# Layer 0's gate with stationary weights in four column groups of TensorE, turned by two transposes

## The chip, the cores and the metric

The kernel runs on one core of one Trainium2 chip. The metric is the device time of one execution in microseconds. The kernel before takes 3072.12 us, the median of three runs (3068.05 to 3079.04).

## What is computed

A stack of four graph layers on 16 graphs of 1024 nodes with 128 features, each followed by a residual addition and a layer norm. The change concerns layer 0, a gated attention over the graph:

```python
h = x @ W_w.T + W_b
e = jnp.einsum('bjl,bkl->bjk', h @ A, h)
e = e + jnp.swapaxes(e, 1, 2)
att = jnp.where(adj > 0, e, jnp.float32(-9000000000000000.0))
att = jax.nn.softmax(att, axis=1) * adj
h_prime = jax.nn.relu(jnp.einsum('bij,bjk->bik', att, h))
coeff = jax.nn.sigmoid(jnp.concatenate([x, h_prime], axis=-1) @ gate_w.T + gate_b)
return coeff * x + (1.0 - coeff) * h_prime
```

The gate `coeff` is one number per node: a dot product of 256 values, 128 of them from the node's input and 128 from its attention result.

## The kernel before, in words

`fast_kernel` runs the layers one after the other: layer 0, the dilation of the adjacency matrices, the three graph convolutions of layer 1, and layers 2 and 3. Layer 0 goes through 16 graphs ("batches"), each in three streams, which `in_turn` interleaves, so that in the steady state three batches are in work at once: `before` of batch b+1, `attention` of batch b, `after` of batch b−1. The tile framework then fixes the order of the instructions on each engine when the program is built; on the chip each engine takes its instructions in that order, and semaphores hold an instruction until what it needs is there.

`before` (line 891 on) has eight steps, one for each block of 128 adjacency rows `an`. ScalarE casts the block and sums it (`ab`, line 900), VectorE checks it (`chk`, line 903, in a buffer of its own of 1024 bytes per partition), TensorE turns it by eight transposes (`pt`, line 907), and VectorE writes it as a mask (`carry`, line 908). Between these steps come the products: the turned input `xT` (step 1), `hT` from `W0T` and the gate's first half `pz` with its copy `gx` (step 3), `G` (step 5), `hn` (step 7).

`attention` (line 933 on) has eight steps jt: a mask on ScalarE (`msk`, line 942), the scores `pmm` on TensorE (line 723), mask and maximum on VectorE (`em`, line 945), the exponential on ScalarE (line 949), `rs` and `hs` on VectorE (lines 951 and 953), and `acc` on TensorE (line 956).

`after` (line 959 on) forms `hpT`, the ReLU of `acc`, on ScalarE, then the gate's second half `pz` (line 965), adds `gx` (`co`, line 967), takes a tanh, and mixes input and result (`xn`, `r`, lines 974 to 977), before the layer norm (lines 777 to 784, with a power on GpSimd at line 744).

The gate's product has the node features stationary and the weight vector moving: for each of the eight blocks of 128 nodes, one matmul loads 128x128 float32 values and streams a single column. It gives 128 nodes on the partitions and 8 columns, which is how `co` is used.

`ps_h` is a pool of PSUM with two buffers under the one tag "h". The products, `pt`, the turned tiles and the gate all take turns in it: the third tile waits until the first is read. `ps_w` has two buffers for the scores `pmm`, `ps_a` one for `acc`.

`bad` (line 675) collects the dilation's flags, which are 0 or 1; the end of the kernel takes their maximum.

Of the kernel before, what the change touches and what calls it, by code (L numbers as in the profile page):

```python
# [9 lines left out]
F32 = mybir.dt.float32  # L10
F16 = mybir.dt.float16
F32R = mybir.dt.float32r
BF16 = mybir.dt.bfloat16
I32 = mybir.dt.int32
I8 = mybir.dt.int8
FP8 = mybir.dt.float8e4
# [6 lines left out]
P = 128  # L23
# [616 lines left out]
def fast_kernel(ctx: ExitStack, tc: tile.TileContext, t: dict, out: bass.AP, flag: bass.AP):  # L640

    nc = tc.nc
    B, N, D = t["x"].shape
    NT = N // P
# [3 lines left out]
    consts = ctx.enter_context(tc.tile_pool(name="consts", bufs=1))  # L648
    dram = ctx.enter_context(tc.tile_pool(name="dram", bufs=1, space=DRAM))

    identf = consts.tile([P, P], F32, name="identf")
# [20 lines left out]
    deg = consts.tile([P, BT], F32, name="deg")  # L672
    dinv = deg

    bad = consts.tile([P, 2, NT, B], F32, name="bad")
    past = consts.tile([P, NT - 2, B], F32, name="past")
    other = consts.tile([P, BT], F32, name="other")

# [82 lines left out]
    def products(psum, *pairs):  # L761

        for p, c, _ in halves(psum):
            for i, (W, x) in enumerate(pairs):
                nc.tensor.matmul(p, W, x[:, c], start=(i == 0), stop=(i == len(pairs) - 1))  # L765
            yield p, c

    def half_rows(v):

        return v[:, :, None].to_broadcast([P, 4, P])  # L770
# [97 lines left out]
    with ExitStack() as ph:  # L868

        early = ph.enter_context(tc.tile_pool(name="l0_early", bufs=1, reuse_waits="tile"))  # L870
        wts = ph.enter_context(tc.tile_pool(name="l0_w", bufs=1, reuse_waits="tile"))
        ps_w = ph.enter_context(tc.tile_pool(name="l0_pw", bufs=2, space=PSUM, reuse_waits="tile"))
        ps_a = ph.enter_context(tc.tile_pool(name="l0_pa", bufs=1, space=PSUM, reuse_waits="tile"))
        ps_h = ph.enter_context(tc.tile_pool(name="l0_ph", bufs=2, space=PSUM, reuse_waits="tile"))

        with tc.tile_pool(name="l0_raw", bufs=1) as raw:
            W0T = transposed(wts, ps_h, matrix(raw, t["L0_gnn_W_w"], "l0W"), "l0WT", "h")
            As0 = symmetric(wts, ps_h, matrix(raw, t["L0_gnn_A"], "l0A"), "l0As", "h")
        work = ph.enter_context(tc.tile_pool(name="l0_work", bufs=1, reuse_waits="tile"))
        small = ph.enter_context(tc.tile_pool(name="l0_small", bufs=2, reuse_waits="tile"))  # L880
        b0 = column(wts, t["L0_gnn_W_b"], "l0b")
        gw = wts.tile([P, 2], F32, name="l0gw")
        with nc.allow_non_contiguous_dma(reason="a vector of 256"):
            nc.sync.dma_start(gw, t["L0_gnn_gate_w"].rearrange("o (h d) -> d (o h)", d=P))
        gb = row_bcast(wts, t["L0_gnn_gate_b"], 1, "l0gb")
        gbh = wts.tile([P, 1], F32, name="l0gbh")
        nc.vector.tensor_scalar(gbh, gb, 0.5, None, op0=OP.mult)
        nbig = wts.tile([P, 1], F32, name="l0nbig")
        nc.vector.memset(nbig, -BIG)

        def before(s, b):

            s.xn = work.tile([P, NT, P], F32, name="xn", bufs=3)
            nc.sync.dma_start(s.xn, nat(t["x"][b]))
            for it in range(NT):
                c = b * NT + it
                an = early.tile([P, N], F32, name="an", bufs=2)
                nc.sync.dma_start(an, t["adj"][b][it * P:(it + 1) * P, :])
                ab = early.tile([P, N], BF16, name="ab", bufs=2)
                nc.scalar.activation(ab, an, AF.Copy, accum_out=deg[:, c:c + 1])  # L900

                chk = early.tile([P, N], FP8, name="chk")
                nc.vector.scalar_tensor_tensor(chk, an, 0.0, an, op0=OP.is_gt, op1=OP.not_equal,  # L903
                                               accum_out=other[:, c:c + 1], saturate=False)
                pt = ps_h.tile([P, NT, P], BF16, name="pt", tag="h")
                for jt in range(NT):
                    nc.tensor.transpose(pt[:, jt, :], ab[:, jt * P:(jt + 1) * P], identb)  # L907
                nc.vector.tensor_scalar(Y[b][:, :, it * P:(it + 1) * P], pt, 0.0, None, op0=OP.is_gt, saturate=False)  # L908
                if it == 1:
                    xT = early.tile([P, N], F32, name="xT")  # L910
                    for p, c, _ in turned(ps_h, s.xn):
                        nc.scalar.copy(xT[:, c], p)
                elif it == 3:
                    s.hT = work.tile([P, N], F32, name="hT", bufs=2)
                    for p, c in products(ps_h, (W0T, xT)):
                        nc.scalar.activation(s.hT[:, c], p, AF.Identity, bias=b0)
                    pz = ps_h.tile([P, NT], F32, name="pz", tag="h")
                    for i in range(NT):
                        nc.tensor.matmul(pz[:, i:i + 1], xT[:, i * P:(i + 1) * P], gw[:, 0:1], start=True, stop=True)
                    s.gx = small.tile([P, NT], F32, name="gx")  # L920
                    nc.vector.tensor_copy(s.gx, pz)
                elif it == 5:
                    s.G = work.tile([P, N], F32, name="G", bufs=2)
                    for p, c in products(ps_h, (As0, s.hT)):
                        nc.scalar.copy(s.G[:, c], p)
                elif it == 7:
                    s.hn = work.tile([P, N], F32, name="hn")
                    for p, c, _ in turned(ps_h, s.hT):
                        nc.vector.tensor_copy(s.hn[:, c], p)
                yield  # L930
            nc.gpsimd.dma_start(adj8_d[b], Y[b].bitcast(F32))

        def attention(s, b):


            s.acc = ps_a.tile([P, N], F32, name="acc")
            for jt in range(NT):
                js = slice(jt * P, (jt + 1) * P)
                c = b * NT + jt
                mx = mx0[:, c:c + 1]  # L940
                msk = work.tile([P, N], BF16, name="msk", bufs=2)
                nc.scalar.activation(msk, Y[b][:, jt, :], AF.Identity, scale=BIG, bias=nbig)  # L942
                e = wide_matmul(ps_w, s.hT[:, js], s.G)
                em = work.tile([P, N], F32, name="em", bufs=2)
                nc.vector.tensor_tensor_reduce(em, e, msk, 1.0, -3.0e38, op0=OP.add, op1=OP.max, accum_out=mx)  # L945
                nmx = small.tile([P, 1], F32, name="nmx")
                nc.vector.tensor_scalar(nmx, mx, -1.0, None, op0=OP.mult)  # L947
                sm = small.tile([P, 1], F32, name="sm")
                nc.scalar.activation(em, em, AF.Exp, bias=nmx, accum_out=sm)  # L949
                rs = small.tile([P, 1], F32, name="rs")  # L950
                nc.vector.reciprocal(rs, sm)
                hs = small.tile([P, P], F32, name="hs")
                nc.vector.tensor_scalar(hs, s.hn[:, js], rs, None, op0=OP.mult)  # L953
                for h in range(H2):
                    c = slice(h * 512, (h + 1) * 512)
                    nc.tensor.matmul(s.acc[:, c], hs, em[:, c], start=(jt == 0), stop=(jt == NT - 1))  # L956
                yield

        def after(s, b):

            hpT = work.tile([P, N], F32, name="hpT")
            nc.scalar.activation(hpT, s.acc, AF.Relu)
            pz = ps_h.tile([P, NT], F32, name="pz", tag="h")
            for i in range(NT):
                nc.tensor.matmul(pz[:, i:i + 1], hpT[:, i * P:(i + 1) * P], gw[:, 1:2], start=True, stop=True)
            co = small.tile([P, NT], F32, name="co")
            nc.vector.tensor_add(co, pz, s.gx)
            nc.scalar.activation(co, co, AF.Tanh, scale=0.5, bias=gbh)
            cx = small.tile([P, NT], F32, name="cx")
            nc.vector.tensor_scalar(cx, co, 0.5, 1.5, op0=OP.mult, op1=OP.add)  # L970
            nc.vector.tensor_scalar(co, co, -0.5, 0.5, op0=OP.mult, op1=OP.add)
            yield
            r = work.tile([P, NT, P], F32, name="r")
            nc.vector.tensor_mul(s.xn, s.xn, per_row(cx))
            for p, c, k in turned(ps_h, hpT):
                nc.vector.tensor_mul(r[:, k, :], tiles3(p), half_rows(co[:, k]))
            nc.vector.tensor_add(s.xn, s.xn, r)
            yield
            normed(small, s.xn)
            nc.gpsimd.dma_start(nat(x1_d[b]), s.xn)  # L980
            yield

        in_turn(before, attention, after)
# [712 lines left out]
```

## Time and profile before

| what | value |
|---|---|
| time, median of 3 | 3072.12 us |
| profiled span | 3066.2 us |
| PE, DVE, ACT busy over the span | 93%, 76%, 66% |
| gate of line 919, matmuls | 256 x 245 ns, 29.5 us |
| gate of line 965, matmuls | 256 x 247 ns, 30.0 us |
| `gx` and `co` on VectorE | 16 each, 167 ns |
| layer 0 | about the first 760 us |

PE is TensorE's matmuls and PEld its weight loads, DVE VectorE, ACT ScalarE, POOL GpSimd. A row of the profile names the line, the engine, the tile that is written and the tiles that are read. [...] A float32 matmul appears as two loads and two matmuls. The chain of work that ended last shows each piece with its start and its share of the chain, without overlap.

### The profile page before, as it was taken

How to read it: one execution, taken by the hardware profiler on the slowest of the kernel's cores; microseconds unless marked ns; L12 is line 12 of the kernel's file. 1: busy time of each engine (PE TensorE's matmuls, PEld its weight loads, DVE VectorE, ACT ScalarE, POOL GpSimd, SP SyncE). 2: the span in 40 equal slices, each digit the busy share in tenths (PEclk: the TensorE clock that was granted, in tenths of full speed). 3: DMA queues.
4: the chain of work that ended last, by engine and by line, in shares of the span. 5: the costliest groups of instructions: out<-in, count | busy, mean ns of one | idle time of the engine just before them, and what ended most of it. 6: DMA issues, size and time to landing. Idle time of an engine off the chain costs nothing.

```text
span 3066.2 us, 43116 instructions
## 1 busy us (share of the span) xinstructions
PE 2848.6 (93%) x15379; PEld 1834.6 (60%) x15442; DVE 2327.7 (76%) x5971; ACT 2015.0 (66%) x3393; POOL 314.6 (10%) x292
## 2 busy tenths in 40 slices
PE   7999999997899999999999987999999999999995
PEld 4454554554566566777788874555655555555554
DVE  7788888886899996676678885766667677767765
ACT  6677777775678877565555534766666666666753
POOL 0000000003000001111122231000000000000000
PEclk9999999998899999999999997999999999999997
DMA  5344344331000014223366793111121121111000
GB/s 188 117 139 149 132 138 151 131 131 49 2 2 2 1 79 162 83 93 122 122 218 226 251 331 113 35 56 62 55 69 55 63 74 63 55 55 56 21 14 22
DMA packets 123216, 297.98 MB, mean 97 GB/s; under 512 B 12656, under 2 KB 64624, under 8 KB 115824
## 3 DMA queue, kind: packets, MB, share of 16 engines
q1 hardware_dynamic: 102384, 211.13, 20.6%
q0 software_dynamic: 20608, 84.00, 7.4%
q8 instruction: 124, 2.03, 0.3%
q14 instruction: 100, 0.82, 0.1%
HBM read 211.04 MB, written 84.02 MB: 96 GB/s over the span
## 4 chain that ended last, share of the span: by engine, by line
PE 60%; issue 17%; DVE 13%; ACT 3%; POOL 3%; DMA 3%; SPq 0%; POOLq 0%; DVEq 0%; ACTq 0%
PE pmm L723 10%; PE acc L1272 9%; PE ph L1515 7%; PE ph L765 6%; PE acc L1578 6%; PE acc L956 5%; PE ph L758 4%; PE ph L1376 4%; PE ph L1501 2%; POOL ln_rstd L744 2%; DVE ln_st L777 2%; PE acc L1249 2%; ACT xn L784 1%; DVE chk L903 1%; PE pt L907 1%
## 5 line engine op out<-in xcount | busy, mean ns | idle before, releaser
L723 PE MATMUL pmm<-G,hT 128*128 128x512 f32 x1024 | 518.9, 624 | 17.0 <-DVE mx L945 14.7
L723 PEld LDWEIGHTS pmm<-G,hT 128*128 128x128 f32 x1024 | 182.1, 198 | 180.6 <-issue 113.6
L1578 PE MATMUL acc<-em,hs 128*128 128x512 f32 x512 | 255.2, 610 | 12.1 <-DVE hs L1575 10.5
L956 PE MATMUL acc<-em,hs 128*128 128x512 f32 x512 | 239.0, 603 | 23.7 <-DVE hs L953 22.4
L784 ACT ACTIVATE xn<-xn,ln_nb,ln_rstd 128x128 f32<-128x128 f32 x512 | 206.4, 481 | 79.7 <-DVE ln_nb L782 79.7
L1272 PE MATMUL acc<-a,lo 128*128 128x512 f32 x768 | 241.1, 398 | 2.0 <-DVE lo L1240 2.0
L1272 PE MATMUL acc<-a,hi 128*128 128x512 f32 x768 | 241.8, 399 | 1.2 <-ACT hi L1239 0.9
L744 POOL TENSOR_TENSOR ln_rstd<-ln_rstd,mhalf 128x8 f32<-128x8 f32 x64 | 105.4, 1647 | 1295.2 <-DVE ln_rstd L741 1224.6
L1121 ACT ACTIVATE q<-s,negc 128x512 f16<-128x512 f32 x256 | 170.6, 697 | 58.4 <-DVE negc L1100 22.3
L1119 PE MATMUL s<-step,carry 128*128 128x384 bf16 (+3 forms) x1034 | 199.0, 303 | 7.5 <-DVE carry L1089 3.2
L1564 DVE CUSTOM_DVE_ANT_0 em<-pmm,msk 128x1024 f32<-128x1024 f32 x128 | 156.0, 1219 | 50.2 <-PE pmm L723 47.5
L1133 ACT ACTIVATE carry<-pc,negone 128x512 fp8e4<-128x512 f32 x256 | 166.8, 699 | 37.1 <-PE pc L1132 27.8
L903 DVE SCALAR_TENSOR_TENSOR chk<-an 128x1024 fp8e4<-128x1024 f32 x128 | 156.2, 1220 | 38.3 <-DMA an<-in_adj 37.7
L900 ACT ACTIVATE ab<-an 128x1024 bf16<-128x1024 f32 x128 | 134.6, 1052 | 74.9 <-PE pt L907 36.1
L956 PEld LDWEIGHTS acc<-em,hs 128*128 128x128 f32 x512 | 93.5, 191 | 140.8 <-issue 104.9
L1559 ACT ACTIVATE msk<-A,nbig 128x1024 bf16<-128x1024 fp8e4 x128 | 146.0, 1141 | 47.9 <-DVE mx L1564 46.0
L942 ACT ACTIVATE msk<-carry,l0nbig 128x1024 bf16<-128x1024 fp8e4 x128 | 145.5, 1140 | 46.0 <-DVE mx L945 41.5
L908 DVE TENSOR_SCALAR carry<-pt 128x1024 fp8e4<-128x1024 bf16 x128 | 155.9, 1220 | 23.6 <-PE pt L907 23.5
L1272 PEld LDWEIGHTS acc<-a,lo 128*128 128x128 f32 x768 | 142.8, 188 | 42.9 <-DVE lo L1240 9.5
L1272 PEld LDWEIGHTS acc<-a,hi 128*128 128x128 f32 x768 | 141.6, 188 | 34.0 <-ACT hi L1239 1.4
L945 DVE CUSTOM_DVE_ANT_0 em<-pmm,msk 128x1024 f32<-128x1024 f32 x128 | 155.4, 1214 | 5.4 <-PE acc L956 3.3
L949 ACT ACTIVATE em<-em,nmx 128x1024 f32<-128x1024 f32 x128 | 145.9, 1140 | 17.3 <-DVE nmx L947 13.5
(278 smaller groups left out, 6519.9 us busy)
## 6 DMA issues: line engine op xcount, KB each, us to landing
an<-in_adj SPq DMA_DIRECT2D x128, 512.0 KB, 3.3
adj_d<-carry POOLq DMA_DIRECT2D x16, 1024.0 KB, 4.9
A<-dil_d SPq DMA_DIRECT2D x16, 1024.0 KB, 6.5
rdeg<-rdeg_d SPq DMA_DIRECT2D x32, 512.0 KB, 4.3
ag_d<-ag POOLq DMA_DIRECT2D x32, 512.0 KB, 5.3
ag<-ag_d SPq DMA_DIRECT2D x32, 512.0 KB, 6.2
A<-adj_d SPq DMA_DIRECT2D x16, 1024.0 KB, 4.8
xn<-in_x SPq DMA_DIRECT2D x16, 512.0 KB, 3.7
```

Of the source, the lines that this page charges most:

```text
L723: nc.tensor.matmul(p[:, h * 512:(h + 1) * 512], lhsT, rhs[:, h * 512:(h + 1) * 512], start=True, stop=True)
L744: nc.gpsimd.tensor_tensor(r, r, mhalf[:, :n], op=OP.pow)
L765: nc.tensor.matmul(p, W, x[:, c], start=(i == 0), stop=(i == len(pairs) - 1))
L784: nc.scalar.activation(r[:, i, :], r[:, i, :], AF.Identity, scale=rstd[:, i:i + 1], bias=nb[:, i:i + 1])
L903: nc.vector.scalar_tensor_tensor(chk, an, 0.0, an, op0=OP.is_gt, op1=OP.not_equal, accum_out=other[:, c:c + 1], saturate=False)
L956: nc.tensor.matmul(s.acc[:, c], hs, em[:, c], start=(jt == 0), stop=(jt == NT - 1))
L1119: nc.tensor.matmul(s[:, lo or 0:], y, twos if lo is None else step[:, :512 - lo], start=(j == 0), stop=(j == len(terms) - 1))
L1121: nc.scalar.activation(q[:, h * 512:(h + 1) * 512], s, AF.Abs, bias=st.negc[:, i:i + 1])
L1133: nc.scalar.activation(Y[b][:, hb, ks], pc, AF.Relu, bias=negone, saturate=False)
L1272: nc.tensor.matmul(acc, part[:, jt, :], pieces[h * NT // 2 + i][:, j, :], start=(jt == 0 and p == 0), stop=(jt == NT - 1 and p == 1))
L1515: nc.tensor.matmul(p, part[:, jt, :], A[:, jt, c], start=(jt == 0 and i == 0), stop=(jt == NT - 1 and i == 1))
L1578: nc.tensor.matmul(s.acc[:, c], hs, em[:, c], start=(jt == 0), stop=(jt == NT - 1))
```

## The change

The gate is turned around. Its weight vector becomes the stationary operand: `gw` grows from two columns to two blocks of 32 columns, of which the first holds the weights and the others are zero. The features become the moving operand. The new helper `gates` gives each quarter of the 1024 nodes to one column group of TensorE, by `tile_position`: four matmuls of 32 stationary columns and 256 moving columns write to partitions 0, 32, 64 and 96 of one PSUM tile (`pq`). ScalarE copies that tile to SBUF; two transposes bring the nodes back to the partitions (`pg`), and `gx` and `co` read column 0 of each group. The copy takes the buffer of `chk` in `before` and that of `r` in `after`, and `bad` becomes bfloat16, so that no more SBUF is needed.

It is meant to replace eight loads of 128x128 stationary values, each for one moving column, by four matmuls side by side.

```diff
-    bad = consts.tile([P, 2, NT, B], F32, name="bad")
+    bad = consts.tile([P, 2, NT, B], BF16, name="bad")
...
+    def gates(psum, out, *pairs):
+        p = psum.tile([P, N // 4], F32, name="pq", tag="h")
+        for i, (g, x) in enumerate(pairs):
+            for q in range(4):
+                nc.tensor.matmul(p[32 * q:32 * q + 32, :], g, x[:, q * N // 4:(q + 1) * N // 4], start=(i == 0),
+                                 stop=(i == len(pairs) - 1), tile_position=(0, 32 * q))
+        nc.scalar.copy(out, p)
+        p = psum.tile([P, 2, P], F32, name="pg", tag="h")
+        for t in range(2):
+            nc.tensor.transpose(p[:, t, :], out[:, t * P:(t + 1) * P], identf)
+        return p.rearrange("p t (q g) -> p q t g", q=4)
...
-        gw = wts.tile([P, 2], F32, name="l0gw")
+        gw = wts.tile([P, 2, 32], F32, name="l0gw")
+        nc.vector.memset(gw, 0.0)
...
-                    pz = ps_h.tile([P, NT], F32, name="pz", tag="h")
-                    for i in range(NT):
-                        nc.tensor.matmul(pz[:, i:i + 1], xT[:, i * P:(i + 1) * P], gw[:, 0:1], start=True, stop=True)
+                    pz = gates(ps_h, early.tile([P, N], FP8, name="chk").bitcast(F32), (gw[:, 0, :], xT))
                     s.gx = small.tile([P, NT], F32, name="gx")
-                    nc.vector.tensor_copy(s.gx, pz)
+                    nc.vector.tensor_copy(s.gx.rearrange("p (q t) -> p q t", t=2), pz[:, :, :, 0])
...
-            pz = ps_h.tile([P, NT], F32, name="pz", tag="h")
-            for i in range(NT):
-                nc.tensor.matmul(pz[:, i:i + 1], hpT[:, i * P:(i + 1) * P], gw[:, 1:2], start=True, stop=True)
+            pz = gates(ps_h, work.tile([P, NT, P], F32, name="r").rearrange("p t d -> p (t d)")[:, :N // 4], (gw[:, 1, :], hpT))
             co = small.tile([P, NT], F32, name="co")
-            nc.vector.tensor_add(co, pz, s.gx)
+            nc.vector.tensor_add(co.rearrange("p (q t) -> p q t", t=2), pz[:, :, :, 0],
+                                 s.gx.rearrange("p (q t) -> p q t", t=2))
```

More of the change, by code (lines that the diff above doesn't have):

```diff
@@ L881, in fast_kernel @@
         b0 = column(wts, t["L0_gnn_W_b"], "l0b")
-        gw = wts.tile([P, 2], F32, name="l0gw")
+        gw = wts.tile([P, 2, 32], F32, name="l0gw")
+        nc.vector.memset(gw, 0.0)
         with nc.allow_non_contiguous_dma(reason="a vector of 256"):
-            nc.sync.dma_start(gw, t["L0_gnn_gate_w"].rearrange("o (h d) -> d (o h)", d=P))
+            nc.sync.dma_start(gw[:, :, 0], t["L0_gnn_gate_w"].rearrange("o (h d) -> d (o h)", d=P))
         gb = row_bcast(wts, t["L0_gnn_gate_b"], 1, "l0gb")
```

## The prediction

> **What bounds the kernel now.** The change touches layer 0 only, so I first ask where layer 0 is and what limits it. The answer by windows shows five alike stretches of 100 us between 150 and 650 us, at full TensorE clock:
>
> ```profile
> 250.00:350.00 100.00, 93.86 (x426) 50.57 (x425) 85.82 (x203) 76.21 (x126) 6.88 (x7) 1.00 0.41 140
> 350.00:450.00 100.00, 94.14 (x429) 51.25 (x428) 85.43 (x204) 75.50 (x123) 6.33 (x6) 1.00 0.41 140
> ```
>
> Columns are busy us of PE, PEld, DVE, ACT and POOL. TensorE is 94% busy, VectorE 85%, ScalarE 76%: three engines close together, so what a TensorE saving is worth depends on the waits between them. Next, the chain of work that ended last, for one batch (the gate of line 965 starts at 400.83 and again at 446.02, so a batch takes 45.19 us):
>
> ```profile
> 400.83 1.68 PE pz L965 x16
> 402.51 0.48 PE pt L907 x8
> ...
> 403.01 1.23 DVE carry L908
> ...
> 418.53 1.23 DVE chk L903 x2
> ...
> 420.30 3.67 PE acc L956 x8
> 423.97 1.68 PE pz L919 x16
> 425.65 0.47 PE pt L907 x8
> ...
> 440.58 3.43 PE acc L956 x8
> 444.04 1.98 PE pmm L723 x4
> ```
>
> The reader should see two halves. From 403.0 to 420.3 the chain runs through VectorE; from 420.3 to 446 and on to 403 it is TensorE back to back, and both gates (1.68 us each) stand in that half. The third view is VectorE's waits in the same batch:
>
> ```profile
> DVE chk L903 <- DMA an<-in_adj: 3.1, 3, 1.3
> DVE carry L908 <- PE pt L907: 1.3, 3, 0.8
> DVE gx L921 <- PE pz L919: 1.1, 1, 1.1
> DVE ln_nb L782 <- POOL ln_rstd L744: 0.7, 1, 0.7
> DVE rs L951 <- ACT em L949: 0.5, 2, 0.3
> DVE co L967 <- PE pz L965: 0.4, 1, 0.4
> ```
>
> VectorE waits only 7.1 of 45.19 us, and already 1.5 us of that are for the gates. So both engines are nearly full, and TensorE has little to give before VectorE is the bound.
>
> **What the Trainium skill says.** "TensorEngine Tiling (Array Packing)", section Key Properties: column tiles of 32 can run in parallel, and changing the tiling mode drains TensorE. "TensorE: Matmul & The Clock Gate", section Measured speedup vs the span model: three column groups at 512 columns gave 2.38 times; it also says that matmuls start and end in program order. The same page, section Architectural detail, says VectorE and ScalarE work strictly in order, which agrees with gx above waiting 1.1 us with other work behind it. No row of this trace has a column-tiled matmul of several groups (all large groups are 128*128), so neither the overlap nor the drain is shown here.
>
> **The change, part by part.** Removed per gate: 8 one-column matmuls, which the trace shows as 16 loads and 16 matmuls, 1.68 us of TensorE on the chain; 32 gates, 53.8 us. Each float32 matmul is two passes: two halves of pmm (4 records) take 1.72 us, so a pass of 512 columns takes 0.43 and one of 256 takes 0.215.
>
> Added on TensorE: 4 column groups x 2 passes x 0.215. Bounds: all groups side by side 0.43; all in a row 1.72. Between lies a staircase: the two passes of a group cannot overlap, and as starts are in order, a group can only overlap the last pass of the one before: 5 steps, 1.07. I take the staircase, since the two passes are separate records. Drain into and out of the tiling: a matmul record lasts 0.16 us beyond its 0.43 spacing (0.59 against 0.43); I take 0.2 for each, from 0 to 0.4. Two transposes: four take 0.44 in the chain, so 0.21. Sum per gate 1.04, 1.68 and 2.33 (side by side, staircase, in a row) against 1.68: on TensorE alone −20, 0 and +21 us over 32 gates.
>
> Added on ScalarE: a copy of 128x256 from PSUM. 128x512 takes 0.577 and 128x1024 1.022, which by a straight line gives 0.36; 0.7 per batch on an engine that is a quarter idle. Costed at nothing by itself, but it stands in a chain. VectorE's reads of the gate stay 128x8 (0.17). The memset, the wider weight tile and `bad` in bfloat16 (8-column instructions, other layers) cost nothing visible: the first runs while the first loads land (VectorE waits 3.1 us there), and the others keep their element counts.
>
> What is added is a wait: matmuls, ScalarE copy, transposes, VectorE. In the changed program TensorE does one tile of pmm (1.72) between pq and pg to cover the copy, and instruction order outside layer 0 is unchanged but for a few rows at its seam with the dilation. Behind gx on VectorE stand the chk and carry of the next rows, and behind co the hs which TensorE needs; both queues wait with the gate. The second slot of the two-buffer "h" pool that pg takes is freed by this same read.
>
> **A batch of the changed kernel, walked by hand** with the durations above (VectorE's large instructions follow each other at about 1.17 us), T=0 where hpT is done; three values are side by side, staircase, in a row.
> 1. acc ended at −1.05. One pmm tile ends at 0.67, pq with its drains at 1.5, 2.15, 2.8, the next pmm tile at 3.2, 3.9, 4.5. The copy, behind an exp (1.13) and a msk (1.14), is done by 2.8 to 3.3: hidden. pg and its tail 0.4: co at c = 3.6, 4.3, 4.9. In the kernel before it is at 402.54 − 399.88 = 2.66. VectorE's own work ahead of co lasts till about 3.6, so it waits 0, 0.7, 1.3.
> 2. From c, VectorE does co, hs and the like (1.0), 2 em, 4 carry, 2 xn (8 x 1.17), 2 r (1.24), the statistics (2.1), small ones (1.1), and waits for the power on GpSimd (0.75): c + 15.6. The last carry frees the slot for the second half of W0T (0.86), then acc (1.72): c + 18.3.
> 3. Second gate: pq with drains 0.83, 1.47, 2.12, pmm 1.72, pg 0.4: gx at c + 21.3, 21.9, 22.5. VectorE's work ahead of it ends near c + 20, so it waits 1 to 2.5 us.
> 4. After gx, 6 chk, 4 carry, 2 em (12 x 1.17) and small ones (1.7) up to the last hs: 15.8, with 1.3 of waits for pt and em as now. Then acc and hpT 2.95. TensorE needs c + 36 for its part up to that acc, so VectorE sets the end.
>
> Period: 45.0, 46.2, 47.4, against 45.19. Over 15 batches: −4, +16, +34 us.
>
> **The rivals.** Forecast, partial overlap with VectorE waiting at gx: 3072 + 16 = 3088. Chance 0.37. Rival one, faster: the groups run side by side and VectorE's order has slack that my walk misses (the changed order lets two chk go ahead of co, out of the stretch where VectorE carries the chain), so the full TensorE saving arrives: 3072 − 20 = 3052, and without any drain −33. For it: both gates lie on the chain, in the TensorE half. Against: VectorE's 7.1 us of waits. Chance 0.35. Rival two, no change: side by side, but the longer chain eats it, −4, 3068; chance 0.18. Rival three: no overlap at all, +34, 3106; chance 0.10. It needs the groups to queue, against the skill's figure, which was for other operands.
>
> **How the numbers follow.** Slower 0.37 + 0.10 = 0.47, same 0.18, faster 0.35. My walk may be wrong by 1 us per batch, 15 us. The range goes from 3042, a little short of the drainless saving, to 3110, a little over no overlap.
>
> **What would show it.** Right: pq starts overlap in pairs and four matmuls take 1.0 to 1.5 us; VectorE's wait at gx grows from 1.1 to 2 us or more; the period of a batch is near 46. Wrong: the pq group takes under 0.6 us (rival one or two), or VectorE waits less for the gates than now and the period falls under 44.5. If any other layer's time moves by over 5 us, my view that it stays is wrong.

## The result and the profile after

The changed kernel takes 3049.43 us (median of 4 runs, 3045.44 to 3053.27), the kernel before in the same comparison 3075.58 us. The ratio is 0.9917, 95% interval 0.989 to 0.9944: 26 us faster, where 16 us slower was forecast. The time lies in the range, near rival one (3052).

The views of before again, now for the changed kernel. First the windows (busy us of PE, PEld, DVE, ACT, POOL, then the granted TensorE clock, DMA share, GB/s):

```profile
250.00:350.00 100.00, 92.11 (x396) 45.10 (x394) 86.16 (x205) 78.99 (x130) 6.89 (x7) 0.98 0.44 148
350.00:450.00 100.00, 93.40 (x429) 47.46 (x429) 90.39 (x227) 79.62 (x134) 7.99 (x7) 1.00 0.41 137
```

TensorE is as full as before (92 to 93%), although each gate costs it less: more batches pass in the same time. VectorE goes from 85% to 86 and 90%. The TensorE timeline around one gate (start, us to the end of the last, engine, line):

```profile
409.59 1.02 PE L969 MATMUL acc<-em,hs 128*128 128x512 f32 x2
410.54 0.64 PE L774 MATMUL pq<-xT,l0gw 128*32 128x256 f32 x8
411.11 1.98 PE L723 MATMUL pmm<-G,hT 128*128 128x512 f32 x4
412.93 0.38 PE L779 MATMUL pg<-identf,chk 128*128 128x128 f32 x2
413.15 1.88 PE L969 MATMUL acc<-em,hs 128*128 128x512 f32 x4
414.87 0.33 PE L922 MATMUL pt<-identb,ab 128*128 128x128 bf16 x3
```

A record can last longer than the distance to the next start (in the kernel before, a gate's matmuls last 245 ns and start 106 ns apart), so a cost is read from start to start. From the start of `pq` to the next instruction are 0.57 us, for `pg` 0.22. The passes around `pq` grow too. The last four of `acc` take 1.72 us to the start of `pt` at 414.87, 0.43 each; the two ahead of `pq` take 0.95 (409.59 to 410.54) and the four of `pmm` behind it 1.82 (411.11 to 412.93), so 0.09 and 0.10 us more. In layer 0 the first pass of `pmm` takes 0.53 us in all 30 places where it follows `pq`, and 0.43, as the median of 30, where it follows `acc`. With its surroundings a gate takes 0.57 + 0.22 + 0.19 = 0.98 us of TensorE. In the kernel before, start to next start, it was 1.70 us (16 records of 0.106), and the pass ahead of it kept its 0.43.

How the passes overlap stands in this count of records by slice (the same view, windows of the tile `pq` alone; the first number in brackets counts the matmuls in work, the second the loads):

```profile
410.50:410.60 0.10, 0.06 (x4) 0.06 (x8) 0.00 (x0) 1.00 0.00 0
410.60:410.70 0.10, 0.10 (x4) 0.10 (x8) 0.00 (x0) 1.00 0.00 0
410.70:410.90 0.20, 0.20 (x8) 0.00 (x0) 0.00 (x0) 1.00 0.00 0
```

Four of the eight matmul records are in work within 0.1 us, and the other four start together after 410.7. The records don't name their group; that the first four are the first passes of the four groups is the likely reading. There is no staircase.

VectorE's waits in one batch (390.18 to 432.94, a gate of line 774 to the next):

```profile
DVE em L958 <- PE acc L969: 1.9, 3, 1.4
DVE gx L934 <- PE pg L779: 0.8, 1, 0.8
DVE ln_nb L796 <- POOL ln_rstd L744: 0.7, 1, 0.7
DVE co L978 <- PE pg L779: 0.5, 1, 0.5
```

They fell from 7.1 to 3.9 us: `chk` stands elsewhere in the new order, and its 3.1 us for its data are gone in this batch, those of `carry` too. (Between 250 and 650 us, the rows of `chk` sum to 20.8 us before and 6.8 now.) So two things changed at once, TensorE's time and the order. The chain of work that ended last, over the same batch of the changed kernel:

```profile
409.74 1.15 ACT hT L931 x2
410.88 1.13 ACT em L962 x2
412.01 0.10 ACT chk L776
...
412.16 1.26 ACT em L962 x2
...
413.43 0.12 DVE chk L918
...
420.79 3.41 DMA an<-in_adj
```

No TensorE piece is left in it: it runs through ScalarE (here with the copy of the gate between two exponentials), VectorE and the loads of `an`. Before, it was TensorE back to back for half a batch. The engines stand so close that the chain alone doesn't tell which of the two changes paid. The copy itself takes 0.36 us (rows of line 776, 356 and 360 ns).

Over the layer, the first `hpT` of layer 0 starts at 82.7 us (78.2 before), the last at 722.0 (744.8 before). The start of the layer is 4.5 us later, and the 15 batches between take 639.2 in place of 666.6 us. Over nine batches in the middle the period is 43.73 in place of 45.23 us. The gain is made in layer 0.

The nine are not alike: seven take 42.7 to 43.6 us, two 46.5 and 46.6. One of the long ones and the batch behind it, in the columns of the first view, then TensorE's longest wait in each:

```profile
252.90:299.40 46.50, 41.95 (x182) 20.81 (x181) 38.66 (x92) 35.82 (x61) 3.16 (x3) 0.96 0.45 145
299.40:342.20 42.80, 40.03 (x182) 20.00 (x181) 38.58 (x92) 33.23 (x56) 3.17 (x3) 1.00 0.40 138
```

```profile
PE pt L922 <- ACT G L938: 2.8, 1, 2.8
PE pt L922 <- ACT G L938: 1.3, 1, 1.3
```

In both long batches ScalarE waits 4.9 and 5.0 us for a load of `an` (4.1 in the batch behind), TensorE then waits 2.8 and 2.3 us for the transposes, and next the granted clock falls (0.96 over the batch). The median of the first fourteen stretches from one `hpT` to the next leaves such batches aside: it is 42.8 us, and 45.2 in the kernel before. It is used below, from one profile of each run.

### The profile page after: what moved, and what is told of

Same layout as the page of the kernel before. It is cut to its first block, busy times and chain, and to the rows that moved or that the text cites. A ratio compares the mean times of both kernels' runs of the same rounds, so it can differ in the third digit from the quotient of the medians.

```text
span 3049.5 us, 42855 instructions
## 1 busy us (share of the span) xinstructions
PE 2825.3 (93%) x15187; PEld 1794.2 (59%) x15250; DVE 2325.2 (76%) x5972; ACT 2018.8 (66%) x3425; POOL 315.2 (10%) x292
## 4 chain that ended last, share of the span: by engine, by line
PE 58%; DVE 21%; ACT 9%; DMA 5%; issue 5%; POOL 3%; SPq 0%; POOLq 0%; ACTq 0%; DVEq 0%
PE acc L1284 9%; PE pmm L723 8%; PE ph L1527 7%; PE acc L1590 6%; PE ph L765 6%; PE ph L758 4%; PE ph L1388 4%; DMA an<-in_adj 3%; ACT xn L798 3%; PE s L1131 2%; PE acc L969 2%; POOL ln_rstd L744 2%; PE ph L1513 2%; DVE mid L1085 2%; DVE ln_st L791 2%
## 5 line engine op out<-in xcount | busy, mean ns | idle before, releaser
L723 PEld LDWEIGHTS pmm<-G,hT 128*128 128x128 f32 x1024 | 188.3, 201 | 174.2 <-issue 148.7
L1284 PEld LDWEIGHTS acc<-a,lo 128*128 128x128 f32 x768 | 142.9, 188 | 42.8 <-DVE lo L1252 9.5
L918 DVE SCALAR_TENSOR_TENSOR chk<-an 128x1024 fp8e4<-128x1024 f32 x128 | 156.3, 1221 | 14.0 <-DMA an<-in_adj 13.6
L1388 PE MATMUL ph<-Wx,hT 128*128 128x128 f32 x768 | 152.3, 281 | 4.9 <-DVE l2WT L709 3.2
```

Source lines behind the costliest of these rows:

```text
L723: nc.tensor.matmul(p[:, h * 512:(h + 1) * 512], lhsT, rhs[:, h * 512:(h + 1) * 512], start=True, stop=True)
L1284: nc.tensor.matmul(acc, part[:, jt, :], pieces[h * NT // 2 + i][:, j, :], start=(jt == 0 and p == 0), stop=(jt == NT - 1 and p == 1))
L1388: nc.tensor.matmul(p[:, i * P:(i + 1) * P], x[:, j * P:(j + 1) * P], W, start=(n == 0), stop=(n == 1))
```

## The experiments

Three theories. **One:** TensorE sets the batch, and the gain is its time taken off. **Two:** the new order of instructions, above all of `chk` on VectorE, made the gain. **Three**, the prediction's: VectorE sets the end of a batch. The runs named "order kept" edit the finished list of instructions, so that every engine's order stays as it was; an edit of the source puts layer 0 in a new order, which is a change of its own.

### TensorE time added in the changed kernel, order kept

Each group of four `pq` matmuls is run once more (`more` is 1), or twice more (2), in place:

```diff
...
+                    if len(group) == 4:
+                        for m in range(more):
+                            for j in [group[3]] + group[:3]:
+                                new.append(copy.replace(j, name=f"I-{n}", sync_info=None))
...
```

> The changed kernel with its instruction order kept: on TensorE each group of four gate matmuls is run a second time in place, and nothing else differs. The group takes 0.57 us, so this adds 32 x 0.57 = 18 us of TensorE time. Theory 1 (the gain is TensorE time taken off the path that sets layer 0): 3049 + 18 = 3067 us, and the ratio to the kernel before is near 0.997. Theory 2 (the gain came from the new order of VectorE's work, and TensorE has slack now) and theory 3 (the prediction's: VectorE sets the end of a batch): 3049 to 3054 us, ratio 0.992 to 0.993.

> The same with each group run three times in place: 2 x 0.57 x 32 = 36.5 us more TensorE time than in the changed kernel, so a gate costs TensorE 1.93 us, about what it cost in the kernel before (1.84), but in the changed kernel's order. Theory 1: 3049 + 36 = 3085 us, all of the gain is gone and a little more, ratio 1.003. Theory 2: the gain of the order stays, 3060 us or less, ratio 0.995 or lower. Theory 3: VectorE's waits of 3.9 us per batch take the first part, so at most 3049 + 12 = 3061 us.

The times are 3060.51 us, ratio 0.9942 (0.9924 to 0.996), and 3070.38 us, ratio 0.9975 (0.9962 to 0.9988). The TensorE timelines of the two runs, once more and then twice more, show what was added:

```profile
392.52 1.07 PE L774 MATMUL pq<-hpT,l0gw 128*32 128x256 f32 x16
393.52 0.70 PE L723 MATMUL pmm<-G,hT 128*128 128x512 f32 x1
```

```profile
419.54 1.50 PE L774 MATMUL pq<-xT,l0gw 128*32 128x256 f32 x24
420.97 1.98 PE L723 MATMUL pmm<-G,hT 128*128 128x512 f32 x4
```

To the next instruction are 1.00 and 1.43 us: a repeat costs 0.43, not the 0.57 of my expectation. So the runs add 32 x 0.43 = 13.8 and 27.5 us. Against the changed kernel the ratios say 0.0025 x 3076 = 8 us and 0.0058 x 3076 = 18 us. The intervals of the first overlap; the second is clear (18, give or take 9). Added TensorE time is paid at about 0.6 of its length: theory one in kind, not in full. Theory three's limit of 3061 us for the second run is broken.

The batches show where the rest is. The median batch is 43.9 us with one repeat and 44.6 with two, against 42.8: 1.1 and 1.8 us for the 0.86 and 1.72 that were added. In the median batch TensorE's time is paid in full. But no batch of these two runs has a lowered clock in its profile, and the two that have one in the changed kernel are 3.7 and 3.8 us over its median, 7.5 us in all. The other three runs with the cheap gates in this order (half of the check, and layer 2's two, below) have two or three such batches behind the first as well, of 45.1 to 46.2 us.

In the second run a gate takes 1.43 + 0.22 + 0.19 = 1.84 us, 0.14 more than the 1.70 of before, in the changed kernel's order. (The 1.84 for the kernel before in my expectation is the length to the end of the last record.) It is still 8 us faster than the kernel before (interval 4 to 12). That much at least the order, with all else that came along, gives.

### TensorE time taken off in the kernel before, order kept

The first matmul of a gate writes five columns and four are left out. In short, each line as output, stationary and moving operand:

```diff
-  8 x  pz[:, i] <- xT block i (stationary), gw (1 column)
+  1 x  pz[:, 0:5] <- xT block 0 (stationary), gw (the column five times)
+  3 x  pz[:, i] <- xT block i (stationary), gw (1 column)
```

> The kernel before with its order of instructions kept, and only four of the eight matmuls of each layer 0 gate: the first writes five columns, four are left out, and so the gate of four of the eight blocks of nodes is not computed (block 0's stands in their place). No copy and no transposes. It takes 8 of 16 loads and matmuls, 0.84 us of 1.68, off TensorE 32 times, 27 us. Theory 1: 27 us less than the kernel before, ratio 0.991, the same as the whole change brought. Theory 2 (it was the order): within 5 us of the kernel before, ratio 0.998 to 1.0. Theory 3: VectorE's 7.1 us of waits per batch give some of it, 5 to 12 us, ratio 0.996 to 0.998.

3048.98 us, ratio 0.9912 (0.989 to 0.9933), 27 us faster. Start to next start, a gate takes 0.81 in place of 1.70 us, 28.5 us in all: paid nearly in full, with no copy, no transposes, and the old order. VectorE still waits for its data as before; the waits over 250 to 650 us in this run:

```profile
DVE chk L903 <- DMA an<-in_adj: 26.6, 28, 1.5
```

(20.8 in the kernel before.) So that wait need not go away for the gain to come. Theory two falls as the main cause. With the run above this makes a square of four, each with its ratio, TensorE's time for a gate and the median batch:

| | dear gate | cheap gate |
|---|---|---|
| order of before | 1 (1.70 us, batch 45.2) | 0.9912 (0.81 us, batch 43.7) |
| order of after | 0.9975 (1.84 us, batch 44.6) | 0.9917 (0.98 us, batch 42.8) |

By the whole time, the two orders are worth the same at the cheap gate. TensorE's time is worth 27 us in one order and 18 in the other; the order is worth 8 us with the dear gate and nothing that can be told with the cheap one. By the median batch, TensorE's time is worth 1.5 us in one order (1.78 taken off) and 1.8 in the other (1.72), and the new order is 0.6 and 0.9 us the shorter, although its gates are the dearer. So of the 2.4 us between the two kernels' median batches, the larger part is TensorE's time. At the cheap gate the order's part is lost again in the two long batches (this run has one, of 46.1 us) and in the start of the layer: the first `hpT` comes at 82.7 us, in this run at 76.9.

The same edit on one half of the gate only, then on the other:

> The kernel before with its order kept; only the gate's first half (over the node features) has four of its eight matmuls, the first writing five columns, so the gate of four blocks of nodes is not computed there. 0.89 us of TensorE less per batch, 14 us in 16 batches. Theory 1 (TensorE time is paid in full wherever it stands): 14 us less than before, ratio 0.9954. If instead only one of the two places stands on the path, as the chain of one batch cannot tell: 0 or 27 us, ratio 1.0 or 0.991.

> The same for the gate's second half (over the attention result) alone: 14 us of TensorE less, half of its matmuls left out. Theory 1: ratio 0.9954, and together with the run for the first half the 27 to 29 us of both. If the order decides instead, as the 20 us that the first half alone lost when its instructions were put in order anew suggest: with the order kept there is no loss in either.

3066.82 us, ratio 0.9978 (0.9968 to 0.9989), and 3063.13 us, 0.9963 (0.995 to 0.9977): 7 and 11 us of 14 each. Both places count. Their sum is 18, give or take 5; the run with both had 27 (21 to 34). The intervals overlap.

### VectorE relieved, order kept

```diff
-  chk <- an (128x1024), other (sum of 1024 columns)
+  chk <- an (128x512),  other (sum of 512 columns)
```

> The changed kernel with its order kept, and each check of a block of adjacency rows on VectorE looks at 512 of the 1024 columns (so half of the check is left out). The check of 1024 columns takes 1.22 us; at half I expect about 0.65, so VectorE has some 8 x 0.57 = 4.6 us less to do in each of 16 batches, 73 us. Theory 1 (TensorE sets the batch, VectorE's waits have room): at most 10 us less than 3049, 3039 to 3049 us, ratio to the kernel before 0.988 to 0.992. Theory 3 (the prediction's: VectorE sets the end of a batch): half or more of the 73 us shows, 3013 us or less, ratio 0.98 or lower.

> The kernel before with its order kept and the same half of the check left out, 73 us of VectorE work in all. It says which engine set the batch before the change. Theory 1: at most 15 us less than the kernel before, ratio 0.995 to 1.0. Theory 3: 36 us or more, ratio 0.988 or lower. Theory 2 (order on VectorE mattered before, because a check that waits for its data holds up what is behind it): something between, 8 to 25 us, ratio 0.992 to 0.997.

3048.28 us, ratio 0.9908 (0.9894 to 0.9922), 1 us under the changed kernel's median; and 3069.57 us, 0.9975 (0.9967 to 0.9984), 7 us under the kernel before. The rows of the check, of the changed kernel and then of the run with half:

```profile
L918 DVE SCALAR_TENSOR_TENSOR chk<-an 128x1024 fp8e4<-128x1024 f32 x128 | 156.3, 1221 | 14.0 <-DMA an<-in_adj 13.6
```

```profile
L918 DVE SCALAR_TENSOR_TENSOR chk<-an 128x512 fp8e4<-128x512 f32 x128 | 88.2, 689 | 17.2 <-DMA an<-in_adj 16.5
```

156.3 − 88.2 = 68 us of VectorE work went, and at most a few us came back; the median batch is 42.9 us, against 42.8. Where they went is in VectorE's waits between 250 and 650 us, of the changed kernel and then of the run with half:

```profile
DVE em L958 <- PE acc L969: 20.0, 24, 2.0
...
DVE carry L923 <- PE pt L922: 0.5, 1, 0.5
```

```profile
DVE em L958 <- PE acc L969: 25.7, 26, 2.6
DVE carry L923 <- PE pt L922: 17.4, 18, 2.0
```

VectorE now waits for TensorE instead of working. Theory three falls: an engine that is busy for 86 to 90% with waits of 4 us in a batch did not set the end of it. In the kernel before, 7 of 68 us is a small share too.

### One gate by source

Only the gate's first half turned around, then only the second; the instructions come in a new order each time:

```diff
-  pz = gates(ps_h, early.tile(... "chk") ..., (gw[:, 0, :], xT))      # one run or the other
-  pz = gates(ps_h, work.tile(... "r") ..., (gw[:, 1, :], hpT))
+  for i in range(NT): nc.tensor.matmul(pz[:, i:i + 1], ...)           # as before
```

> Only the gate's first half (over the node features, gx) is turned around; the second half (over the attention result, co) stays as 8 one-column matmuls. The instructions are put in order anew. Theory 1: half of the TensorE saving, 16 x 0.9 = 14 us less than the kernel before, ratio 0.995. Theory 2: depends on what the order does to the checks; with the check behind gx as in the changed kernel most of the gain, ratio 0.992 to 0.994.

> Only the gate's second half (over the attention result, co) is turned around; the first half (over the node features, gx) stays as 8 one-column matmuls. The instructions are put in order anew. Theory 1: half of the TensorE saving, 14 us less than the kernel before, ratio 0.995. Theory 2: the copy here has no part in the check's buffer, so the check keeps its place and little is gained, ratio 0.997 to 1.0.

3098.35 us, ratio 1.0063 (1.0051 to 1.0075), and 3070.24 us, 0.9974 (0.9964 to 0.9984). No theory had a loss of 20 us in the first. TensorE saves 16 x (1.70 − 0.98) = 11.5 us there, so the rest of that program loses 31. Its VectorE waits between 250 and 650 us begin with

```profile
DVE rs L964 <- ACT em L962: 26.2, 24, 2.0
```

a wait for the exponential that the whole change doesn't have near the top (the row `rs` was 4.9 us in the kernel before). In its profile the granted clock is 0.96 in six of the fourteen stretches of 40 us from 100 to 660 us; the six batches with a lowered clock take 47.4 to 48.3 us, seven of the other eight 45.3 to 46.7. These two runs don't divide the gain, since each has its own order. That the order is what costs 31 us is argued: no run has that order with the old gate. What makes ScalarE late there was not followed up.

### The two small edits alone

```diff
-    bad = consts.tile([P, 2, NT, B], F32, name="bad")
+    bad = consts.tile([P, 2, NT, B], BF16, name="bad")
...
-        gw = wts.tile([P, 2], F32, name="l0gw")
+        gw = wts.tile([P, 2, 32], F32, name="l0gw")
+        nc.vector.memset(gw, 0.0)
```

> The kernel before with only the wider weight tile (64 columns, set to zero first) and the flags of the dilation in bfloat16; the gate itself is as before, and the order of instructions too, but for one memset. Every theory: no change, within 3 us, ratio 0.999 to 1.001. Should it gain or lose more, part of the result belongs to these two edits.

3078.42 us, ratio 1.0005 (0.9996 to 1.0013). They cost nothing that can be told from zero, as forecast.

### The same gate in layer 2

```diff
...
-            for i in range(NT):
-                c = slice(i * P, (i + 1) * P)
-                nc.tensor.matmul(pg[:, i, :], s.xT[:, c], gw[:, 0, :], start=True, stop=False)
-                nc.tensor.matmul(pg[:, i, :], hpT[:, c], gw[:, 1, :], start=False, stop=True)
+            pg = gates(ps_h, wide("x3T")[:, :N // 4], (gw[:, 0, :], s.xT), (gw[:, 1, :], hpT))
...
```

> The changed kernel, and layer 2's three gates by the same helper: the two inputs as two pairs, three of the 32 stationary columns used. The gate of a batch there is now 32 loads and 32 matmuls, some 3.4 us of TensorE; it would be two groups of 0.57 and 0.22 for the transposes, 1.36 us, a saving of 2.0 us in each of 16 batches, 32 us. Theory 1 carried over (TensorE sets layer 2 as well): 3049 - 32 = 3017 us, ratio 0.981. If layer 2 is set by ScalarE or VectorE, or if the copy and the transposes stand in a chain there: within 8 us of the changed kernel, or slower, ratio 0.989 or higher.

> The changed kernel with layer 2's gates by the same helper, as in the earlier run, but the copy goes to a buffer of yn, not of x3T; the order of VectorE is that of the earlier run. There TensorE lost its saving to a wait for ehi, 1.7 us in a batch. If the shared buffer x3T delays the turned features and with them ehi: some 15 to 25 us less than the earlier run, 3012 to 3020 us. If the wait belongs to the chain of layer norm and elu that TensorE used to cover: the same as the earlier run, 3033 to 3039 us, ratio 0.985 to 0.987.

3035.76 us, ratio 0.986 (0.984 to 0.988), and 3033.52 us, 0.9865 (0.9849 to 0.9882). Both beat both kernels, by 14 and 16 us against the changed one's median (18 and 16 by the ratios); of the 32 us that the saving on TensorE promised, about half came, and the buffer is not the reason. TensorE's waits over ten batches of layer 2, of the changed kernel and then of the first of these runs, tell where the rest went:

```profile
PE acc L1590 <- DVE hs L1587: 8.1, 10, 0.8
PE ph L758 <- ACT xn L798: 6.3, 10, 0.6
```

```profile
PE ph L1514 <- DVE ehi L1501: 19.0, 10, 2.6
PE ph L758 <- ACT xn L798: 13.6, 10, 2.2
PE pmm L723 <- DVE mx L1577: 3.6, 5, 0.7
PE ph L758 <- DVE zn L1516: 2.2, 5, 0.4
```

The rows grow from 14.4 to over 38 us, 2.4 us in each batch. There TensorE's freed time became a wait for VectorE's `ehi` and ScalarE's `xn`. The waits grew by more than the 2.0 us that the gate was to save, and yet a batch became 0.8 us shorter (71.7 to 70.9). The granted clock over these ten batches is 0.98 in place of 0.96, which may be a part of it; this was not followed up. In layer 0 nothing like this happened: over 250 to 650 us TensorE's three largest waits sum to 29.0 us in the changed kernel (13.9, 11.1, 4.0) and 26.4 us before (14.6, 9.8, 2.0).

## Why the prediction was wrong

The direction was wrong, for two steps that failed one after the other. The walk by hand can be held against two runs: the changed kernel, and the run with each group twice more, whose gate of 1.84 us is dearer than the 1.68 that the forecast assumed. Means over nine or ten batches, the long ones among them, us:

| | walk, side by side | changed kernel | walk, staircase | twice more |
|---|---|---|---|---|
| `co` after hpT (c) | 3.6 | 3.63 | 4.3 | 4.26 |
| VectorE's wait at `gx` | 1.3 | 0.82 | 1.9 | 1.68 |
| from `co` to `gx` | 21.3 | 20.42 | 21.9 | 21.15 |
| from `gx` to the next hpT done | 20.05 | 19.59 | 20.05 | 19.21 |
| batch | 45.0 | 43.64 | 46.2 | 44.63 |

**First failed step: "I take the staircase".** `pq` was put at 1.07 us with drains of 0.2 on each side, 1.47; with its surroundings it takes 0.57 + 0.19 = 0.76. With `pg` (0.22 against the 0.21 forecast) a gate is 0.98 in place of 1.68 us: a term mis-sized by 0.70, 22 us over 32 gates. The value taken was the middle of the bounds; the low bound for the matmuls, 0.43, is what a repeat in place takes. The drains were nearly right: 0.76 − 0.43 = 0.33 us against 0.4. The reason given, that starts in order keep a group from overlapping all but the last pass of the one before it, is refuted by the slices above: four records run together, then the other four. The Trainium skill's sentence on parallel column tiles ("TensorEngine Tiling (Array Packing)", Key Properties) holds here without loss: four groups of two passes take 0.43, in a row they would take 4 x 0.43 = 1.72. Of the drain on a change of mode, which the same section states, these runs leave room for 0.33 us, into and out of the mode together; how much of that is the drain they don't show.

**Second failed step: "TensorE needs c + 36 for its part up to that acc, so VectorE sets the end".** Even at a higher TensorE cost than the forecast assumed, the time is 3070 us and not 3088. The beginning of the walk was right to 0.05 us, and the VectorE waits at `gx` in size too, but the stretches that it summed from VectorE's work came out 0.5 to 0.9 us too long, twice in a batch. The half-check run shows why they must not be summed that way: with six checks, 6 x 0.53 = 3.2 us less on VectorE, between `gx` and the next hpT, that stretch went from 19.59 to 19.78 (medians 19.0 and 19.1). The argument "against" rival one, VectorE's 7.1 us of waits, had no force: a batch overlaps three graphs' work, and VectorE's order had room.

What held: the copy costs 0.36 us and is hidden from TensorE (the pass ahead of `pg` keeps its 0.43), the two transposes 0.22, the small edits nothing, and VectorE does wait for the gates. The tests named ahead of the run decided as they said: `pq` under 0.6 us from its start to the next, waits for the gates of 1.3 us in the batch shown (1.5 before), and a period under 44.5. The last of them, that no other layer moves by over 5 us, can't be judged. From the first to the last `hpT` of layer 2 the profiled kernels with an unchanged layer 2 take 1032.8 to 1043.2 us, the kernel before 1036.1, the changed one 1042.6; one profile of each doesn't tell such a difference from chance.

Rival one was right in its mechanism and nearly in size. Its 20 us took a gate at 1.04 us; at the 0.98 measured, TensorE's saving is 23 us, and the kernel gained 26 (interval 17 to 34).

Still open: what makes the long batches of the changed kernel. By these profiles, their 7.5 us are most of the gap between the 18 us paid for added TensorE time and the 27.5 added. The traces show the order of events in them, a later load of `an`, a longer wait of TensorE, a lowered clock, but no run was made to tell cause from company. In the kernel before and in both runs with repeats, the granted clock is 1.00 in all 14 stretches of 40 us from 100 to 660 us; in the changed kernel it is 0.96 in two of them. I estimate 2 x 40 x 0.04 = 3 us for the clock by itself, under half of that. Why the layer starts 4.5 us later was not followed up either.

## What to carry to other kernels

A product with one or a few output columns can be cheaper with the weights stationary and the output spread over column groups, where the transposes back and the copy can stand behind other work: here 0.98 against 1.70 us. Count what the change does to the instructions on both sides of it: that was 0.19 of the 0.98. To learn which engine sets a stage, take work off one engine with the order of instructions kept and see whether the time follows; sums along one engine misled here. Look at the batches one by one as well: a mean over nine hid two long ones. And when the source is edited, the order is edited too: one half of this change alone, in its own order, was 20 us slower than nothing.

## What the runs showed of the hardware that was not expected

Four column groups run fully side by side in float32: eight matmul records, 128x32 stationary and 128x256 moving, in 0.43 us when they follow the same kind, 0.57 us from their start to other work, and 0.76 with the 0.19 by which the 128x512 passes on both sides grow. The stationary blocks of 32 columns load in 105 to 110 ns each, and all eight loads of a group of four lie within 0.16 us. A matmul with 128x128 stationary values costs no more with five moving columns than with one: four of them, one with five columns, take 0.81 us, 0.101 for each record, against 0.106 with one column throughout. In the changed kernel's layer 0, the granted clock fell twice, each time behind a wait of TensorE of over 2 us, and these batches took 46.5 and 46.6 us, the median one 42.8.
